# A GRU of two layers followed by a mixture of experts on one core: two parts of the shared expert's inner layer are made at the end of the recurrence, the routing is written out in one fixed order, and small edits are made around both

## The chip, the cores and the metric

The kernel runs on one core of one Trainium2 chip. The metric is the device time of one execution, in microseconds. Each core has five engines: PE (TensorE, matmul, with its weight loads shown apart as PEld), DVE (VectorE), ACT (ScalarE), POOL (GpSimd) and SP (SyncE, which here only starts transfers). Each engine works off its own list of instructions in order.

## The reference, cut to what matters

The input x has 2 sequences of 1024 tokens of 256 numbers. Two layers are added to it, one after the other:

```python
ctx   = cond[:, None, :]
mixed = tanh(x @ W_in.T + b_in + ctx)
h2    = gru(gru(mixed, Wih0, Whh0, ...), Wih1, Whh1, ...)
gate  = sigmoid(cond @ W_gate.T + b_gate)
x     = x + (gate[:, None, :] * h2 + h2) @ W_out.T + b_out

xf     = x.reshape(2048, 256)
shared = silu(xf @ w1) * (xf @ w3) @ w2                 # inner width 512
s      = sigmoid(concat([xf, cond of the row]) @ router_W)       # 8 experts
best   = top_k(s + router_bias, 2)
gates  = s[best] / (sum(s[best]) + 1e-9)   (1/2 each where the sum is <= 1e-9)
routed = sum over the two experts e of gates * gelu(xf @ W1e[e]) @ W2e[e]
out    = x + (shared + routed) / 3
```

## The kernel before, in words

**The recurrence.** Each sequence is cut into chunks that are stepped side by side. The program is a row of *ticks*; in each tick both GRU layers make one step (`step`, inside the class that also has `finish_scanned`, L325-371): matmuls with the recurrent weights (L296), a sigmoid on ACT (L341), a scan on DVE (L344), an elementwise operation (L357), a tanh on ACT (L355), a second scan (L360) and a transpose (L369). Each waits for the one before, so other work is placed by hand into the gaps: `place(tick, where, what)` records a piece of work for a tick and a spot in it ("product" and "behind" on PE, "n0", "scan0", "scan1", "end" for the others), and the main loop (L684-747) takes it out there. When the chunk's state from the warm-up steps is to be dropped, a mask `kept` (L337) is made on DVE inside the step; when the real chunk begins, `start_row` (L484) is transposed for both layers. `front.prepare` (L840-900) makes the gate of the reference, and its sums `ps_gate` (L848) stand in one tick. After the last step `fit` (L495-509) checks for each layer that the chunks fit together; the two results are summed and turned into an integer `count` (L761-764) on which a branch for another, sequential computation hangs; that branch is not taken here.

**Between the two parts.** `front.all_of` (L992-1005) makes the output of the GRU for the last group of tokens: `products` (L914) on PE, `add_x` (L925) on DVE, `route` (L941, the router's sums) on PE, then `turn` (L930, transposes) and `keep` (L952, a copy on ACT).

**The mixture of experts** is `moe` (L1008-1376). Its pieces:

- *Ramps and constants* on POOL (L1037-1072).
- *The routing chain* on DVE (L1081-1218): `raw`, `s` (a sigmoid on ACT), `sel`, then twice `top`, `at`, `place`, `first`, `one`; `both`; two matmuls that count (L1112); `upto` and the `slot` of every token; `low` and `high`; `in_block` and `at_lane`, large one-hot tables of float16; 32 matmuls into `few` (L1171); and `pick` (L1179), the list of token numbers for each block of 128 slots. Beside it stand `mine` to `share` (L1202-1218), the weights of the two experts, and `past` to `words` (L1182-1196), the owner of each block.
- *The shared expert's inner layer* in 16 parts (4 blocks of 512 tokens x 4 slices of 128 inner numbers). A part is `hidden_sums` (L961-970) for w1 and for w3, on PE, two matmuls each of 128x512, and `hidden` (L977-983): `sig` on ACT (L981), `silu` on DVE (L982), and `silu` times the w3 sums on DVE (L983). One part is made ahead of the routing: its w1 sums and half of its w3 sums in the last ticks, the other half as `behind` in `all_of`, its last multiplication after that. EARLY = 8 parts stand beside the routing (a scheduler puts their instructions between those of the routing), one part is filled in at the experts' end (FILL), and the last 6 come in the tail.
- *The experts*: 35 blocks (SURE) of 128 slots. For each, POOL starts an indirect DMA that fetches the block's tokens by `pick` (L1274); PE transposes them (L1237), DVE copies the transpose (L1239), PE multiplies by W1e (L1245), ACT applies gelu (L1285), PE transposes and multiplies by W2e, and the result is stored to `back`. The fetch of block i+3 stands three blocks ahead.
- *The tail*, in an order written by hand (L1353-1376): 8 gathers back (L1335) are started at once, each 128 rows of `back`. Then the 6 parts follow, with two more gathers for each; then 16 output tiles `ps_s` (L1367, four matmuls of 128x256 each), with the last gathers. `add_gone` (L1349) adds the gathered rows with their shares, L1375 adds `ps_s`, L1376 stores the tile. Each gather with an even number is held back by a copy of one element on POOL (L1334), which reads something that is made a little earlier.

Of the kernel before, what the change touches and what calls it, by code (L numbers as in the profile page):

```python
# [18 lines left out]
B = 2  # L19
# [51 lines left out]
EARLY = 8  # L71
# [14 lines left out]
def gru_moe(ctx, tc, xT, vec, bias, w_in, wih0, whh0, wih1, whh1, w_out, w_gate, router, w1, w3, w2, w1e, w2e, out):  # L86
# [62 lines left out]
    class Steps:  # L149
# [177 lines left out]
        def finish_scanned(self, layer, to, tick, before_n, after_n, between, keep=None):  # L327
# [7 lines left out]
            if keep is not None:  # L335
                kept = self.edge.tile([P, U], FP, name=f"kept{layer}")
                nc.vector.tensor_scalar(kept, h, keep, -1.0, ALU.mult, ALU.mult)  # L337
                h = kept
# [14 lines left out]
            n = self.step_pool.tile([P, U, 2], FP, name=f"n{layer}")  # L353
            before_n()
# [46 lines left out]
    with ExitStack() as stack:  # L401
        g = Steps(stack, "", on_pe=False, rest_of_x=rest_of_x)
        g.gates = [
# [138 lines left out]

        def let_wait(ins, copied):


            if ins is not None and copied is not None:
                sync = mybir.DependencyInfo(mybir.DependencyClass.Sync, mybir.DependencyReason.DATA)
                tc.add_manual_dep(ins.ins, copied.ins.name, sync, reason="the next product adds to it")
# [48 lines left out]
        places = {}  # L597

        def place(tick, where, what):
            places.setdefault((tick, where), []).append(what)  # L600

# [42 lines left out]
        place(last_tick - 1, "end", silu)  # L644
        for block in range(1, N // MB):
            place(block, "end", lambda block=block: spread(block))
# [4 lines left out]
        for i, todo in enumerate(front.prepare(g.bank)):  # L651
            for where, what in todo.items():
                place(AHEAD[0] - 8 + i, where, what)
# [32 lines left out]
        with tc.manual_schedule():  # L686
            for tick in range(AHEAD[0] + S + LAG):
                now = [layer for layer in range(2) if runs(layer, tick)]
                for layer in now:
                    if layer not in g.states:  # L690
                        g.states[layer], g.rows[layer] = zero_state, zero_row
                    elif position(layer, tick) == 0:
                        g.starts[layer] = g.states[layer] = begin[layer]
                        g.start_rows[layer] = g.rows[layer] = turned(g.starts[layer], f"start_row{layer}")
# [49 lines left out]
                for layer in now:  # L744
                    if position(layer, tick) == S - 1:
                        fits.append(fit(layer))

            for where in ("n0", "scan0", "end"):
                placed(AHEAD[0] + S + LAG, where)
            front.all_of(  # L750
                g.bank,
                GROUPS // GS - 1,
                lambda: begin_hidden("w3", [1]),
                lambda: nc.vector.tensor_tensor(
                    front.hid(0, slice(0, TB)), begun["silu"], begun["w3"], ALU.mult
                ),
# [13 lines left out]
    with tc.If(n_fit < P):  # L770
        with ExitStack() as stack:
# [46 lines left out]
            front.hidden(0, 0, *(front.hidden_sums(g.bank, 0, 0, name)[0] for name in ("w1", "w3")), *temp)  # L818
# [3 lines left out]
class Front:  # L822
# [17 lines left out]
    def prepare(self, bank):  # L840
# [3 lines left out]
        def gate_sums():  # L844
            ps["gate"] = bank("ps_gate")[:, 0 : KD * B].rearrange("p (k b) -> p k b", b=B)
            for m in range(KD):
                for k in range(KD):
                    last = nc.tensor.matmul(  # L848
                        out=ps["gate"][:, m, :],
                        lhsT=later["w_gate"][:, k, m * P : (m + 1) * P],  # L850
                        rhs=vec_sb[:, COND + k * B : COND + (k + 1) * B],
                        start=(k == 0),
                        stop=(k == KD - 1),
                    )
# [36 lines left out]
        def keep_context():  # L891
# [3 lines left out]
            {"product": gate_sums, "scan1": lambda: spread(0)},  # L895
            {"n0": gates, "scan1": lambda: spread(1)},
# [95 lines left out]
    def all_of(self, bank, group, between=lambda: None, behind=lambda: None):  # L992
# [7 lines left out]
        behind()  # L1000
# [9 lines left out]
def moe(ctx, tc, tag, front, out):  # L1010
# [70 lines left out]
    iota = expert.unsqueeze(1).to_broadcast([P, NT, E])  # L1081
    raw = rt("raw")
    nc.vector.tensor_tensor(raw, logits[:, :, 0:E], context.unsqueeze(1).to_broadcast([P, NT, E]), ALU.add)
    s = rt("s")
    nc.scalar.activation(s, raw, AF.Sigmoid)
    sel = rt("sel")
    nc.vector.tensor_tensor(sel, s, vec_sb[:, RBIAS : RBIAS + E].unsqueeze(1).to_broadcast([P, NT, E]), ALU.add)
    chosen = []
    for i in range(2):
        top = rt(f"top{i}", NT, 1)  # L1090
        nc.vector.tensor_reduce(top, sel, AX.X, ALU.max)
        at = rt(f"at{i}")
        nc.vector.tensor_tensor(at, sel, wide(top), ALU.is_equal)

        place = rt(f"place{i}")
        nc.vector.scalar_tensor_tensor(place, iota, float(E), at, ALU.subtract, ALU.mult)
        first = rt(f"first{i}", NT, 1)
        nc.vector.tensor_reduce(first, place, AX.X, ALU.min)
        nc.vector.tensor_scalar(first, first, float(E), None, ALU.add)
        one = rt(f"one{i}")  # L1100
        nc.vector.tensor_tensor(one, iota, wide(first), ALU.is_equal)
        chosen.append(one)
        if i == 0:
            rest = rt("rest")
            nc.vector.scalar_tensor_tensor(rest, one, -BIG, sel, ALU.mult, ALU.add)
            sel = rest
    both = rt("both", dtype=BF)
    nc.vector.tensor_tensor(both, chosen[0], chosen[1], ALU.add)


    for to, which in ((ps_all.rearrange("p (e t) -> p e t", e=E), every), (ps_before, before)):
        nc.tensor.matmul(out=to, lhsT=which, rhs=both.rearrange("p t e -> p e t"), start=True, stop=True)  # L1112
    upto = rt("upto", E, NT)
    nc.vector.tensor_tensor_scan(
        upto.rearrange("p e t -> p (e t)"), running.rearrange("p e t -> p (e t)"), ps_all, 0.0, ALU.mult, ALU.add
    )

    whole = rt("whole", E, dtype=I32)
    nc.vector.tensor_scalar(whole, upto[:, :, NT - 1], float(P - 1), None, ALU.add)
    nc.vector.tensor_scalar(whole, whole, -P, None, ALU.bitwise_and)  # L1120
    size = rt("size", E)
    nc.vector.tensor_copy(size, whole)
    end = rt("end", E)
    nc.vector.tensor_tensor_scan(end, adding, size, 0.0, ALU.mult, ALU.add)
    slots_taken = rt("slots_taken", 1, dtype=I32)
    nc.vector.tensor_copy(slots_taken, end[:, E - 1 : E])
    start = rt("start", E)
    nc.vector.tensor_tensor(start, end, size, ALU.subtract)

    slot = rt("slot", E, NT)  # L1130
    nc.vector.tensor_tensor(slot, upto, ps_all.rearrange("p (e t) -> p e t", e=E), ALU.subtract)
    nc.vector.tensor_tensor(slot, slot, ps_before, ALU.add)
    nc.vector.tensor_tensor(slot, slot, start.unsqueeze(2).to_broadcast([P, E, NT]), ALU.add)
    slot_of = rt("slot_of", 2, NT)
    for c in range(2):
        own = rt(f"own{c}")
        nc.vector.tensor_tensor(own, chosen[c], slot.rearrange("p e t -> p t e"), ALU.mult)
        nc.vector.tensor_reduce(slot_of[:, c, :].unsqueeze(2), own, AX.X, ALU.add)
    slots = rt("slots", 2, NT, dtype=I32)
    nc.vector.tensor_copy(slots, slot_of)  # L1140
    block = rt("block", 2, NT, dtype=I32)
    nc.vector.tensor_scalar(block, slots, -P, None, ALU.bitwise_and)
    high = rt("high", 2, NT)
    nc.vector.tensor_copy(high, block)
    low = rt("low", 2, NT)
    nc.vector.tensor_tensor(low, slot_of, high, ALU.subtract)

    in_block = rt("in_block", 2, NT, NB, dtype=F16)
    at_lane = rt("at_lane", 2, NT, P, dtype=F16)
    for c in range(2):  # L1150
        nc.vector.tensor_tensor(
            in_block[:, c, :, :],
            block_start.unsqueeze(1).to_broadcast([P, NT, NB]),
            high[:, c, :].unsqueeze(2).to_broadcast([P, NT, NB]),
            ALU.is_equal,
        )
        nc.vector.tensor_tensor(
            in_block[:, c, :, :],
            in_block[:, c, :, :],
            token.unsqueeze(2).to_broadcast([P, NT, NB]),  # L1160
            ALU.mult,
        )
        nc.vector.tensor_tensor(
            at_lane[:, c, :, :],
            lane.unsqueeze(1).to_broadcast([P, NT, P]),
            low[:, c, :].unsqueeze(2).to_broadcast([P, NT, P]),
            ALU.is_equal,
        )
    for c in range(2):
        for t in range(NT):  # L1170
            nc.tensor.matmul(  # L1171
                out=ps_pick,
                lhsT=at_lane[:, c, t, :],
                rhs=in_block[:, c, t, :],
                start=(c == 0 and t == 0),
                stop=(c == 1 and t == NT - 1),
            )
    pick = rt("pick", NB, dtype=I32)
# [272 lines left out]
```

## Time and profile before

| what | value |
|---|---|
| median of the runs | 537.25 us (535.58, 538.12 and 537.25) |
| the profiled execution's own time | 538.56 us |
| its span in the trace | 536.8 us |
| PE busy | 512.1 us, 95% of the span |
| DVE, ACT, POOL busy | 385.1, 243.6, 76.9 us |
| last transpose of the recurrence (L369) | 361.00 to 361.24 us |
| `raw`, the first operation of the routing (L1083) | 365.56 us |
| `both` (L1108), `upto` (L1114), `pick` (L1179) | 372.68, 373.82, 388.06 us |
| first fetch of the experts (L1274) | 388.55 us |
| first product of the experts (L1245) | 396.70 us |
| first gather back (L1335) | 477.65 us |
| last `ps_s` (L1367) ends | 531.13 us |

All times in the lower rows are counted from the start of the span. PE is busy nearly all the time, which says how long PE worked and not whether it had to: a matmul's record begins when PE takes it, and the granted clock of PE is shown apart, in tenths of the full rate. In a row of the timeline, the first number is the start, the second the length, then come the engine, the line, the operation and its tile; what stands in brackets is the idle time before it and what ended that. A view of windows gives for each stretch the busy microseconds of PE, PEld, DVE, ACT and POOL with their numbers of records, then the mean granted clock, the share of the DMA engines and the rate of transfer.

### The profile page before, as it was taken

How to read it: one execution, taken by the hardware profiler on the slowest of the kernel's cores; microseconds unless marked ns; L12 is line 12 of the kernel's file. 1: busy time of each engine (PE TensorE's matmuls, PEld its weight loads, DVE VectorE, ACT ScalarE, POOL GpSimd, SP SyncE). 2: the span in 40 equal slices, each digit the busy share in tenths (PEclk: the TensorE clock that was granted, in tenths of full speed). 3: DMA queues.
4: the chain of work that ended last, by engine and by line, in shares of the span. 5: the costliest groups of instructions: out<-in, count | busy, mean ns of one | idle time of the engine just before them, and what ended most of it. 6: DMA issues, size and time to landing. Idle time of an engine off the chain costs nothing. (4 is left out here: it accounts for less than half of the span.)

```text
span 536.8 us, 18511 instructions
## 1 busy us (share of the span) xinstructions
PE 512.1 (95%) x7492; PEld 341.2 (64%) x7492; DVE 385.1 (72%) x1296; ACT 243.6 (45%) x833; POOL 76.9 (14%) x124
## 2 busy tenths in 40 slices
PE   7999999999999999999999999989999999999795
PEld 4556766666665545665665666654458888854584
DVE  3665789999888888888888888888953333336372
ACT  3444355655665656656666565641133333341000
POOL 1200000000000000000000000002064444037570
PEclk9999999999999999999999999999999999999888
DMA  8980000000000000000000000001024443223252
GB/s 283 373 259 2 2 3 4 3 4 2 4 32 3 12 1 4 2 23 22 3 23 2 23 22 4 22 21 61 1 88 128 120 125 123 70 72 104 81 177 85
DMA packets 23103, 32.13 MB, mean 60 GB/s; under 512 B 3056, under 2 KB 18544, under 8 KB 22992
## 3 DMA queue, kind: packets, MB, share of 16 engines
q1 hardware_dynamic: 17344, 19.94, 11.0%
q0 software_dynamic: 3216, 8.79, 5.8%
q10 hardware_dynamic: 2448, 2.11, 1.2%
q8 instruction: 63, 1.03, 0.8%
q14 instruction: 32, 0.26, 0.2%
HBM read 21.26 MB, written 9.57 MB: 57 GB/s over the span
## 5 line engine op out<-in xcount | busy, mean ns | idle before, releaser
L296 PE MATMUL ps_step<-whh_sb,h 128*32 128x192 f32 x3616 | 193.3, 331 | 5.4 <-DVE h L369 4.2
L296 PEld LDWEIGHTS ps_step<-whh_sb,h 128*32 128x32 f32 x3616 | 94.6, 109 | 71.4 <-DVE h L369 51.9
L360 DVE TENSOR_TENSOR_SCAN row<-gates,n 128x128 f32<-128x128 f32 x230 | 98.0, 426 | 29.6 <-ACT n L355 28.3
L344 DVE TENSOR_TENSOR_SCAN ps_step<-gates,ps_step 128x128 f32<-128x128 f32 x230 | 97.3, 423 | 15.0 <-ACT gates L341 15.0
L268 PE MATMUL ps_step<-wih_sb,h 128*32 128x192 f32 x1696 | 99.7, 328 | 4.1 <-ACT ps_step L526 2.4
L355 ACT ACTIVATE n<-ps_step 128x64 f32<-128x64 f32 x228 | 53.0, 232 | 111.0 <-DVE ps_step L344 110.9
L341 ACT ACTIVATE gates<-ps_step 128x128 f32<-128x128 f32 x230 | 66.5, 289 | 35.5 <-PE ps_step L296 26.0
L268 PEld LDWEIGHTS ps_step<-wih_sb,h 128*32 128x32 f32 x1696 | 57.4, 110 | 26.8 <-ACT ps_step L526 14.5
L369 DVE STREAM_TRANSPOSE h<-row 128x64 f32<-128x64 f32 x230 | 56.5, 246 | 8.0
L969 PE MATMUL ps_w<-x_sb,w_sb 128*128 128x512 f32 x128 | 57.3, 597 | 0.2 <-PEq L1320 0.2
L268 PE MATMUL ps_in<-wih_sb,h 128*32 128x192 f32 x1024 | 54.4, 328 | 1.8 <-ACT h L257 1.4
L1239 DVE COPY hT<-ps_hT 128x256 f32<-128x256 f32 x35 | 14.9, 425 | 49.0 <-PE ps_hT L1237 47.1
L526 ACT COPY ps_step<-inputs 128x256 f32<-128x256 f32 x123 | 47.8, 389 | 0.0
L357 DVE SCALAR_TENSOR_TENSOR n<-gates,row 128x64 f32<-128x64 f32 x224 | 47.0, 210 | 0.0
L268 PEld LDWEIGHTS ps_in<-wih_sb,h 128*32 128x32 f32 x1024 | 34.0, 110 | 14.6 <-issue 4.6
L526 ACT COPY ps_step<-bt 128x256 f32<-128x256 f32 x106 | 39.9, 376 | 3.3
L1274 POOL DMA_INDIRECT inputs<-given,pick x35 | 33.3, 951 | 55.2 <-PE ps_xT L1237 31.9
L969 PEld LDWEIGHTS ps_w<-x_sb,w_sb 128*128 128x128 f32 x128 | 23.6, 190 | 27.1 <-issue 24.7
L1245 PE MATMUL ps_h<-w1e_sb,xT 128*128 x140 | 36.1, 380 | 0.7 <-DVE xT L1239 0.7
L1245 PE MATMUL ps_y<-w2e_sb,hT 128*128 x140 | 36.0, 380 | 0.0
L1335 POOL DMA_INDIRECT inputs<-back,slots x32 | 30.9, 964 | 30.0 <-issue 28.3
L1245 PEld LDWEIGHTS ps_y<-w2e_sb,hT 128*128 128x128 f32 x140 | 26.4, 190 | 4.8 <-DVE hT L1239 1.3
(179 smaller groups left out, 430.9 us busy)
## 6 DMA issues: line engine op xcount, KB each, us to landing
back<-y SPq DMA_DIRECT2D x35, 128.0 KB
w1e_sb<-in_w1e SPq DMA_DIRECT2D x1, 2048.0 KB
w2e_sb<-in_w2e SPq DMA_DIRECT2D x1, 2048.0 KB
given<-inputs SPq DMA_DIRECT2D x8, 256.0 KB
out_dram<-inputs ACTq DMA_DIRECT2D x16, 128.0 KB
whh_sb<-in_whh SPq DMA_DIRECT2D x2, 768.0 KB
x_sb<-in_xT SPq DMA_DIRECT2D x3, 512.0 KB
w_sb<-in_w SPq DMA_DIRECT2D x3, 512.0 KB
```

The source lines that it names most:

```text
L268: last = nc.tensor.matmul(out=out[cols(q), :, :], lhsT=given(k), rhs=self.wih[layer][:, k, q * 3 * U : (q + 1) * 3 * U].rearrange("p (g u) ...
L296: nc.tensor.matmul(out=by_sum(self.sums[layer])[cols(q), 0:3, :], lhsT=self.states[layer][:, k, :], rhs=self.whh[layer][:, k, q * 3 * U : ...
L341: nc.scalar.activation(gates[:, :, :, 1], sums[:, 1:3, :], AF.Sigmoid)
L344: nc.vector.tensor_tensor_scan(s, gates[:, 0, :, :].rearrange("p u i -> p (u i)"), ps[:, 0 : 6 * U : 3], 0.0, ALU.mult, ALU.add,)
L355: nc.scalar.activation(n[:, :, 0], s[:, 1 : 2 * U : 2], AF.Tanh, scale=-1.0 if keep is None else keep)
L357: nc.vector.scalar_tensor_tensor(n[:, :, 1], gates[:, 1, :, 1], 1.0, h, ALU.subtract, ALU.mult)
L360: nc.vector.tensor_tensor_scan(row.rearrange("p u i -> p (u i)"), gates[:, 1, :, :].rearrange("p u i -> p (u i)"), n.rearrange("p u i -> p ...
L369: nc.vector.transpose(to, row)
L526: return nc.scalar.copy(by_sum(banks[layer][tick % 2])[:, 0:4, :], g.sum_bias[1] if layer else inputs[:, group_of(0, tick), :, :],)
L969: last = self.tc.nc.tensor.matmul(out=ps, lhsT=self.later[name][:, k, m * P : (m + 1) * P], rhs=self.x1[:, k, blk * TB : (blk + 1) * TB], ...
L1245: nc.tensor.matmul(out=ps, lhsT=of[:, k, :], rhs=weights_sb[:, bass.ds(e * KD + k, 1), :], start=(k == 0), stop=(k == KD - 1),)
L1274: nc.gpsimd.indirect_dma_start(out=xg, out_offset=None, in_=given[:, :], in_offset=bass.IndirectOffsetOnAxis(ap=pick[:, i : i + 1], axis=0),)
```

## The change

1. **Two parts of the inner layer are made ahead of the routing.** EARLY is 6 and the list of parts begins with the third. Of the first part, the second half of the w3 sums goes into the last tick, and its last multiplication right behind the loop. Of the second part, the first half of the w1 sums stands `between` the output's products and `route`; the rest follows `all_of`, behind the check `fit(1)`, which moves from right behind the last step to behind `all_of`. Six parts stand beside the routing, one at the experts' end and seven in the tail.
2. **The routing and the six parts stand in one hand-written order.** In it ACT makes `sig` and a copy `other` of the w3 sums, DVE makes `silu`, and POOL multiplies `silu` by `other` (on DVE before). `past` to `words` stand behind `pick`. In the source `mine` to `share` stand behind the experts.
3. **Every gather back** from the ninth on is held back by the copy of one element, not only each second one.
4. **In the recurrence**, `kept` is made in a scan slot of the tick before, the transpose `start_row` between two operations of the step, and the sums `ps_gate` are split over two ticks, with `prepare` one tick earlier.

```diff
-EARLY = 8
+EARLY = 6
...
-            if keep is not None:
-                kept = self.edge.tile([P, U], FP, name=f"kept{layer}")
-                nc.vector.tensor_scalar(kept, h, keep, -1.0, ALU.mult, ALU.mult)
-                h = kept
...
+            if h is self.turned_row.get(layer):
+                nc.vector.transpose(h, self.states[layer])
             before_n()
...
+        place(AHEAD[0] - FIRST - 2, "scan1", lambda: mask(0))
+        place(AHEAD[0] + LAG - FIRST - 1, "scan0", lambda: mask(1))
...
+        place(last_tick, "behind", lambda: begin_hidden("w3", [1]))
...
-                place(AHEAD[0] - 8 + i, where, what)
+                place(AHEAD[0] - 9 + i, where, what)
...
-                    if position(layer, tick) == S - 1:
-                        fits.append(fit(layer))
+                    if layer == 0 and position(0, tick) == S - 1:
+                        fits.append(fit(0))
...
-            front.all_of(
-                g.bank,
-                GROUPS // GS - 1,
-                lambda: begin_hidden("w3", [1]),
-                lambda: nc.vector.tensor_tensor(
-                    front.hid(0, slice(0, TB)), begun["silu"], begun["w3"], ALU.mult
-                ),
+            nc.vector.tensor_tensor(front.hid(0, slice(0, TB)), begun["silu"], begun["w3"], ALU.mult)
+
+            def begin_next():
+                begun["next"], _ = front.hidden_sums(g.bank, 0, 1, "w1", None, [0])
+
+            front.all_of(g.bank, GROUPS // GS - 1, begin_next)
+            fits.append(fit(1))
+            front.hidden_sums(g.bank, 0, 1, "w1", begun["next"], [1])
+            pb, _ = front.hidden_sums(g.bank, 0, 1, "w3")
+            front.hidden(
+                0,
+                1,
+                begun["next"],
+                pb,
...
-        def gate_sums():
+        def gate_sums(m):
...
-            {"product": gate_sums, "scan1": lambda: spread(0)},
-            {"n0": gates, "scan1": lambda: spread(1)},
+            {"product": lambda: gate_sums(0), "scan1": lambda: spread(0)},
+            {"product": lambda: gate_sums(1), "scan1": lambda: spread(1)},
+            {"n0": gates},
...
+    def look(i):
+        factors[i] = [wk.tile([P, TB], FP, name=name) for name in ("sig", "silu", "other")]
+        nc.scalar.activation(factors[i][0], begun[i, "w1"], AF.Sigmoid)
+        nc.scalar.copy(factors[i][2], begun[i, "w3"])
+
+    def silu_of(i):
+        (blk, m), (sig, silu, other) = parts[i], factors[i]
+        nc.vector.tensor_tensor(silu, begun[i, "w1"], sig, ALU.mult)
+        nc.gpsimd.tensor_tensor(front.hid(m, slice(blk * TB, (blk + 1) * TB)), silu, other, ALU.mult)
+
+    with tc.manual_schedule():
+        sums_of(0)
...
+            if i == 0:
...
+                look(0)
+                sums_of(1)
+                silu_of(0)
...
+        look(1)
+        sums_of(2)
...
+        silu_of(1)
...
+        look(2)
+        sums_of(3)
...
+            silu_of(2 + c)
+            if c == 0:
+                look(3)
+                sums_of(4)
+        sums_of(5, ("w1",), [0])
...
+        nc.vector.tensor_scalar(pick, ps_pick, float(N - 1), None, ALU.min)
+        look(4)
+        silu_of(4)
+        sums_of(5, ("w1",), [1])
+        sums_of(5, ("w3",))
...
+        look(5)
+        silu_of(5)
+
+    shared_hidden(parts[6:EARLY])
...
-        if behind is not None and i % 2 == 0:
+        if behind is not None:
             nc.gpsimd.tensor_copy(yb[0:1, 0:1], behind[0:1, 0:1])
```

## The prediction

> **What bounds the kernel now.** I read the page's head and its slices first.
>
> ```profile
> PE 512.1 (95%) x7492; PEld 341.2 (64%) x7492; DVE 385.1 (72%) x1296; ACT 243.6 (45%) x833; POOL 76.9 (14%) x124
> PE   7999999999999999999999999989999999999795
> PEclk9999999999999999999999999999999999999888
> ```
>
> PE is busy everywhere, but for two thirds of the span it works inside the recurrence, where DVE's chain sets the pace. The slices show two weak places: the one near slice 28 (about 380 us) and the last three, where the clock is lower too. The chain of waits comes next, here without its first and last pieces:
>
> ```profile
> 476.11 20.84 PE ps_w L969 x48
> 496.95 6.26 PE ps_s L1367 x29
> 503.21 0.46 issue
> ...
> 506.26 1.65 issue
> 507.90 23.23 PE ps_s L1367 x94
> 531.13 0.02 issue
> ```
>
> So the tail ends on PE: 48 records of the inner layer (6 parts), then the output tiles. Between 503 and 508 us PE does little though nothing that it needs is named. The windows of the tail show what follows:
>
> ```profile
> 496.00:504.00 8.00, 7.54 (x34) 6.11 (x33) 0.99 (x2) 0.60 (x1) 5.96 (x8) 1.00 0.35 98
> 504.00:508.00 4.00, 1.30 (x6) 0.82 (x5) 2.15 (x5) 0.00 (x0) 2.09 (x2) 0.83 0.34 100
> 508.00:512.00 4.00, 4.00 (x10) 2.98 (x10) 3.25 (x9) 0.00 (x0) 1.29 (x2) 0.50 0.19 66
> 512.00:516.00 4.00, 4.00 (x16) 3.36 (x16) 3.89 (x10) 0.00 (x0) 3.12 (x5) 0.81 0.60 181
> ```
>
> After the gap the granted clock is 0.50. Sixteen tiles of 1.73 us (8 records at 0.216) would be done at 496.95 + 27.7 = 524.6; they are done at 531.13. This **stall** costs 6.5 us. I do not know its cause: ACT's last `sig` waits 6.7 us for sums that PE took up five microseconds earlier. POOL starts gathers without a pause through that time (5.96 of 8 us busy), but it did so before 494 us without harm.
>
> Last, the timeline of the join of the two layers:
>
> ```profile
> 361.39 2.02 PE L914 MATMUL ps_x<-h,gated_out 128*128 128x128 f32 x16 [1.29 <-DVE h L369]
> 365.56 0.29 DVE L1083 TENSOR_TENSOR raw<-logits,context 128x128 f32<-128x128 f32 x1
> 388.06 0.19 DVE L1179 TENSOR_SCALAR pick<-few 128x39 int32<-128x39 f32 x1
> 388.55 1.18 POOL L1274 DMA_INDIRECT inputs<-given,pick  x1 [19.99 <-DVE pick L1179]
> 396.70 1.13 PE L1245 MATMUL ps_h<-w1e_sb,xT 128*128 x4 [0.68 <-DVE xT L1239]
> ```
>
> The routing takes 22.5 us on DVE, and PE has 8 parts (8 x 3.43 = 27.4 us) to do beside it. PE is done with them at 394.99, when the first fetch has long landed (fetches land 2.3 to 2.7 us after their issue). So **PE's work**, not the routing, starts the experts at 396.70. From there to 476 PE is full (75.96 of 76 us), 2.17 us a block.
>
> **The change part by part.** PE's work stays the same to the matmul; it is moved. So I count idle time of PE.
>
> *Recurrence.* `ps_gate` takes PE 1.05 us at 160.83, and the next step's matmuls begin at 161.81 instead of about 161.43: split in two it fits, 0.4 saved. `kept` (0.21 on DVE, twice, between the transpose and the scan) holds the scan by some 0.13, the two `start_row` transposes (0.20 and 0.24) by about 0.1 each, and they move into gaps. Together -0.8, bounds 0 (other work is displaced) and -1.2 (all of their lengths).
>
> *Last tick.* PE idles 1.29 us before `ps_x`. The second half of the w3 sums (1.02) fits in there and not, as before, between products and `route`; the first half of the second part's w1 sums takes its old place. Products and `route` (364.20) stay; 0.9 us of PE's work is gained.
>
> *Ahead of the routing.* DVE gets `fit(1)` (361.28 to 362.48 before, 1.2 us) between the router's sums and the rest, and behind it `silu` and the product of the second part. PE ends the second part's w1 sums at about 366.1 and its w3 sums at 367.8; `sig` 0.60 and `silu` 0.68 are done by 367.4, the product (0.68) by 368.5. `raw` stands behind it on DVE, and so do the ramps on POOL: **368.55 instead of 365.56, 3.0 later**. Who waits: the whole routing.
>
> *The routing.* From `raw` to `both` it took 7.12 us. Two operations of 128x512 leave that stretch (0.6 each by the steps between starts): 5.9, so `both` at 374.5. In the source `mine` to `share` go behind the experts; in the built program's order they still stand on DVE, nine of them between `both` and `upto`. At about 0.2 each they are past the two counting matmuls (0.7) by 0.8, and `upto` starts near 376.4. From there to `low` the operations hang on each other, 0.28 to 0.33 apart, with one `silu` among them: 4.85, so 381.25. Two pairs of `in_block` (0.72 and 0.72) and `at_lane` (2.2) with a `silu` between give 7.9, the last pick matmuls 0.56: **`pick` at 390.4 instead of 388.06, 2.3 later**. The `past` operations (about 1.1) leave the stretch; that is counted.
>
> *PE beside it.* It has 6 parts. It is through with what stands before the last pick matmuls at 387.1, waits 2.6 us for `at_lane`, and ends the sixth part at 392.8.
>
> *POOL.* This is the part that the profile shows least. POOL takes over the last multiplication of six parts, and four of them stand ahead of the first fetch, the fifth between the first and the second. No row shows this multiplication; nearest is POOL's scaling of a tile of the same 128x512 numbers, with one tile read instead of two:
>
> ```profile
> L204 POOL TENSOR_SCALAR wih_sb<-wih_sb 128x512 f32<-128x512 f32 x1 | 1.5, 1502 | 3.7 <-DMA wih_sb<-in_wih 3.7
> ```
>
> Bounds: 0.68 (what DVE takes) and 3.0 (each tile read at that price). I take 1.5, the nearest row. The fourth starts when its `silu` is done at 390.2, so the first fetch is issued near 392.1 (388.55 before), lands at 394.6; the fifth multiplication puts the second fetch at 395.2, landed at 397.5, and PE needs both blocks transposed before its first product: **398.5 instead of 396.70, +1.8**. With 0.68 and a chain 2 us quicker than I count it is 394.0 (-2.7); with 3.0 each, 402.7 (+6.0). What a DVE operation loses beside POOL is 0.1 to 0.2 in the rows around 367 us (`at` 0.37, elsewhere 0.28) and is inside these bounds.
>
> The Trainium skill's page "SBUF — State Buffer", section "Who interferes with whom", says that a DVE operation with two SBUF inputs and a POOL operation that reads SBUF lock each other out for whole instructions. By that rule each of the three multiplications that stand beside `at_lane` and `in_block` would push the chain by up to its own length, and the sum would be some 4 us higher.
>
> *The clock.* PE now idles 2.6 us before 389.7 and about 5.5 us between 392.8 and 398.5, apart from a few transposes. The row of 504 to 508 us is the only one like it: 1.30 of 4 us busy, and half the clock for the next 6.8 us (506.66 to 513.48), which costs 3.4 us where PE is the bound. Bounds 0 and 3.4. Whether the idle time is long and pure enough is open; I take 1.0.
>
> *Tail.* One part more, PE bound: 8 records at 0.43, **+3.4**. The copy for each gather: gathers then stand 1.43 apart instead of 1.35 in the mean. POOL's row of 32 gathers would end 1.5 + 10 + 24 x 1.43 + about 5 = 50.6 us after its first, PE (7 parts and 16 tiles) after 24.0 + 27.7 = 51.7. So PE's work covers it with 1 us to spare: nothing. Without that cover each 0.08 more per gather costs 2 us. The stall I leave as it is; bounds -6.5 (gone) and +3 (half as much again).
>
> *Sum*, against the profiled execution (span 536.8, own time 538.56): -0.8 + 1.8 + 1.0 + 3.4 = +5.4, a span of 542.2 and a time of 544.0. The profiled execution lies 1.3 above the median of the runs; on the median, 537.25 + 5.4 = **542.7 us**. In a sentence: the tail gets a part back, and the time won for it before the experts is lost in PE's waiting for fetches.
>
> **The rivals.**
>
> *The stall goes* (ends on the other side). Place: 494 to 514 us. For it: POOL's gathers came in bare pairs, and every one now waits for work that is done; the parts there are shifted by 3 us too. Against it: the spacing in the mean hardly changes. Price -6.5: 536.2, or 535.2 if the clock holds. From 5.4 us of relief on, the change is no slower.
>
> *The routing ends earlier than counted*: POOL's multiplication is near 0.68 and the hand order saves more. For it: before, 21 of 23 us of DVE are busy between 364 and 387, and six products leave it. Against it: `raw` is 3 us later, and the long one-hot tables (7.3 us) stay. Then the experts start at 394.0: 542.7 - 4.5 - 1.0 = 537.2. Together with the stall's end: 530.7.
>
> *POOL and DVE hinder each other*, or POOL's product takes 3.0: the first product at 402.7, and the clock falls: 542.7 + 4.2 + 2.4 = 549.3.
>
> **How the numbers follow.** About 0.5%, 2.7 us, is what a measurement can tell from no change: faster is below 534.6, slower above 539.9. My forecast 0.39 (its own range 540 to 545.5); the stall goes alone 0.18 (0.10 faster, 0.08 same); the routing quicker alone 0.10 (0.02 faster, 0.05 same, 0.03 slower); both 0.13 (faster); POOL hinders 0.20 (slower). So faster 0.25, same 0.13, slower 0.62. The range 531 to 549 takes in nearly all of the forecast and of the rivals that stand alone.
>
> **What would show it.** In the changed kernel: `raw` near 368.5, `pick` near 390.4, POOL's multiplications at 1.5 us, the first fetch near 392, the first product near 398.5, all less 0.8; the granted clock below 1.00 just behind 398; 56 records of the inner layer in the tail; and a gap of PE with ACT's `sig` waiting some 5 to 7 us in the last 40 us. I am wrong if the experts start before 396, if the tail has no such gap, or if a multiplication on POOL takes over 2 us.

## The result, and the profile after

The changed kernel takes 543.87 us in the median of five runs (543.68 to 544.51), the one before 537.25 in five runs beside them (535.58 to 538.83): ratio 1.0118, 95% interval 1.0098 to 1.0139: slower by 1.2%. The profiled execution has a span of 542.1 us; 542.7 was forecast for the median and 542.2 for the span. One thing has to be known for what follows: the runs were made in groups, and the kernel before itself took 536 to 538 us in three of them and 531.7 to 531.9 in two others. So each ratio below holds for its group (the changed kernel itself ran in the first alone), and absolute times are compared only where that is said.

The page's slices after the change, against those shown for before:

```profile
PE   7999999999999999999999999999689999989995
PEclk9999999999999999999999999999979999999999
```

The weak place near slice 28 is now deeper (6 and 8, where it was 9 and 8), the clock drops there, and the tail's three digits went from 795 to 995: the end has lost its gap, the middle has gained one. The chain of waits (start, length, what) says the same of the end:

```profile
483.51 24.27 PE ps_w L992 x56
507.79 7.55 PE ps_s L1430 x35
...
515.35 1.10 PE ps_s L1430 x4
516.46 0.32 issue
516.78 19.46 PE ps_s L1430 x89
```

Seven parts (56 records) take 24.27 us, and sixteen tiles end at 536.24, which is 0.75 us later than without any gap. Before, the same sixteen tiles lost 6.5. The timeline of the join shows where the middle gets late:

```profile
360.51 2.02 PE L937 MATMUL ps_x<-h,gated_out 128*128 128x128 f32 x16 [0.39 <-DVE logits L979]
367.68 0.29 DVE L1137 TENSOR_TENSOR raw<-logits,context 128x128 f32<-128x128 f32 x1
372.11 1.38 POOL L1131 TENSOR_TENSOR inputs<-silu,other 128x512 f32<-128x512 f32 x1 [1.43 <-ACT other L1126]
372.27 1.36 DVE L1147 TENSOR_TENSOR at<-rest,top 128x128 f32<-128x128 f32 x1
...
379.97 1.28 POOL L1131 TENSOR_TENSOR inputs<-silu,other 128x512 f32<-128x512 f32 x1 [6.48 <-DVE silu L1130]
380.14 0.29 DVE L1198 TENSOR_REDUCE slot_of<-own 128x16 f32<-128x128 f32 x1
380.35 1.13 DVE L1197 TENSOR_TENSOR own<-one,slot 128x128 f32<-128x128 f32 x1
...
387.55 1.33 POOL L1131 TENSOR_TENSOR h<-silu,other 128x512 f32<-128x512 f32 x1 [6.30 <-DVE silu L1130]
387.79 1.75 DVE L1219 TENSOR_TENSOR in_block<-in_block,token 128x624 f16<-128x624 f16 x1
...
392.49 1.27 POOL L1131 TENSOR_TENSOR h<-silu,other 128x512 f32<-128x512 f32 x1 [3.61 <-DVE silu L1130]
392.55 0.20 DVE L1246 TENSOR_SCALAR pick<-few 128x39 int32<-128x39 f32 x1 [0.21 <-PE few L1238]
...
393.93 1.22 POOL L1315 DMA_INDIRECT inputs<-given,pick  x1 [0.17 <-issue]
...
400.76 1.62 PE L1286 MATMUL ps_h<-w1e_sb,xT 128*128 x3 [0.94 <-DVE xT L1280]
```

`ps_x` and `raw` come where they were forecast (367.68 for 368.55 less 0.8). From there the first three of POOL's multiplications each have a DVE row beside them that is 0.8 to 1.1 us too long (`at`, `own`, `in_block`), while `slot_of`, which reads one tile and not two, keeps its 0.29 us beside the second. `pick` is 3 us later than forecast, and the first product comes at 400.76, 4.1 us later than before. What PE waited for between 386 and 486 us (total, times, longest):

```profile
PE few L1238 <- DVE at_lane L1225: 4.4, 1, 4.4
PE ps_w L992 <- DVEq L1383: 1.4, 1, 1.4
PE ps_xT L1278 <- DMA inputs<-given,pick: 1.4, 2, 1.0
PE ps_h L1286 <- DVE xT L1280: 0.9, 1, 0.9
PE ps_y L1286 <- DVE hT L1280: 0.4, 1, 0.4
```

First the tables of the routing, then the fetches. The windows (busy PE, PEld, DVE, ACT, POOL, then the granted clock) show what the waiting does to the clock:

```profile
386.00:392.00 6.00, 1.64 (x25) 0.94 (x24) 5.96 (x6) 1.18 (x2) 1.33 (x1) 0.87 0.01 4
392.00:398.00 6.00, 5.64 (x23) 2.25 (x20) 5.22 (x9) 0.90 (x2) 4.84 (x5) 0.56 0.10 22
398.00:404.00 6.00, 4.05 (x13) 2.96 (x14) 1.27 (x3) 1.95 (x3) 5.02 (x5) 0.72 0.29 87
```

PE is busy 1.64 of 6 us, and the clock halves twice: for most of 392 to 398, and again at the start of the experts.

### The profile page after: what moved, and what is told of

It reads as the page before. It is cut to its first block, busy times and chain, and to the rows that moved or that the text cites. A ratio compares the mean times of both kernels' runs of the same rounds, so it can differ in the third digit from the quotient of the medians.

```text
span 542.1 us, 18554 instructions
## 1 busy us (share of the span) xinstructions
PE 513.3 (95%) x7492; PEld 341.3 (63%) x7492; DVE 389.2 (72%) x1290; ACT 247.4 (46%) x839; POOL 88.7 (16%) x142
## 3 DMA queue, kind: packets, MB, share of 16 engines
q8 instruction: 63, 1.03, 0.8%
## 5 line engine op out<-in xcount | busy, mean ns | idle before, releaser
L992 PE MATMUL ps_w<-x_sb,w_sb 128*128 128x512 f32 x128 | 59.9, 618 | 1.4 <-DVEq L1383 1.4
L1286 PE MATMUL ps_h<-w1e_sb,xT 128*128 x140 | 37.6, 392 | 0.9 <-DVE xT L1280 0.9
L1398 POOL DMA_INDIRECT inputs<-back,slots x32 | 32.2, 1006 | 29.3 <-issue 26.6
L1326 ACT ACTIVATE he<-ps_h 128x256 f32<-128x256 f32 x35 | 13.5, 385 | 36.4 <-PE ps_h L1286 33.5
```

The lines of the kernel that those rows point to most:

```text
L992: last = self.tc.nc.tensor.matmul(out=ps, lhsT=self.later[name][:, k, m * P : (m + 1) * P], rhs=self.x1[:, k, blk * TB : (blk + 1) * TB], ...
L1286: nc.tensor.matmul(out=ps, lhsT=of[:, k, :], rhs=weights_sb[:, bass.ds(e * KD + k, 1), :], start=(k == 0), stop=(k == KD - 1),)
```

## The experiments

Each is told with its edit and with what was put down before it ran. Ratios are those against the kernel before in the same group of runs.

**POOL's multiplication put back on DVE** (a_dve):

```diff
-        nc.gpsimd.tensor_tensor(front.hid(m, slice(blk * TB, (blk + 1) * TB)), silu, other, ALU.mult)
+        nc.vector.tensor_tensor(front.hid(m, slice(blk * TB, (blk + 1) * TB)), silu, other, ALU.mult)
```

> The changed kernel, with the last multiplication of the six parts beside the routing on DVE again (still from the copy that ACT makes). Theory C (beside POOL's multiplication a DVE operation with two inputs stands still: at, own and the multiplication of in_block took 1.36, 1.13 and 1.75 us instead of 0.28, 0.37 and 0.80; and POOL's list holds the first two fetches): at, own and in_block go back to their short times, pick comes at 391.5 to 392 (three multiplications of 0.6 take the place of 2.8 lost), the first fetch at once behind it near 392.2 instead of 393.9, the first product near 397.2 instead of 400.8, the time 539 to 540.5 us. Theory D (the long rows have another cause, and the start of the experts hangs on the chain of DVE alone): pick 1.8 later near 394.4, first product near 400, time 543 to 544 us.

Measured: 540.80 us, ratio 1.0052 (1.0035 to 1.0069) against 1.0118. The timeline, with POOL empty:

```profile
373.30 0.29 DVE L1147 TENSOR_TENSOR at<-rest,top 128x128 f32<-128x128 f32 x1
...
387.77 0.81 DVE L1219 TENSOR_TENSOR in_block<-in_block,token 128x624 f16<-128x624 f16 x1
...
392.09 0.19 DVE L1246 TENSOR_SCALAR pick<-few 128x39 int32<-128x39 f32 x1
...
392.57 1.18 POOL L1315 DMA_INDIRECT inputs<-given,pick  x1 [21.92 <-DVE pick L1246]
```

`at` is back from 1.36 to 0.29 us and the multiplication of `in_block` from 1.75 to 0.81. Theory C holds: three multiplications on DVE cost the chain less than what it lost beside POOL. `pick` is just 0.5 us earlier, but the first fetch follows at once and the second is at 394.06 and not at 396.62; the first product is at 398.19, 2.6 us earlier, where 3.6 was expected. The time lies just above the 539 to 540.5 us of theory C: behind nine fetches in a row (392.57 to 402.82) PE then waits 1.81 us at 404 for its own results, which the experiments on late sums below come back to.

**The shares moved for real** (a_share). In the changed kernel the lines from `mine` to `share` stand behind the experts in the source, and their instructions between `both` and `upto`. Here the block stands inside the hand-written order:

```diff
         nc.vector.tensor_copy(words, word.rearrange("p w i -> p (w i)"))
+        mine = rt("mine", 2, NT)
...
+        nc.vector.tensor_scalar(share, share, 1.0 / 3.0, None, ALU.mult)
```

> The changed kernel, with the operations mine to share moved in the source to right behind words, so that they really stand behind pick on DVE. Theory E (nine to eleven of them hold upto by 0.8 to 1.2 us): upto near 375.8 instead of 376.9, pick and the first product 0.8 to 1.2 earlier, 542.8 us. Theory F (the chain has slack there, POOL's multiplications decide): the first product within 0.3 of 400.8, 543.9 us.

Measured: 542.19 us, ratio 1.0072 (1.0055 to 1.0089). `upto` at 375.42, `pick` at 390.96, the first product at 399.31: 1.45 us earlier than in the changed kernel, of which 0.4 lies ahead of the routing. Theory E holds, at the upper end of its size.

**The copies ahead of the gathers**, taken out of the changed kernel (a_unpaced) and put into the kernel before (b_paced), by the same line:

```diff
-        if behind is not None and i % 2 == 0:
+        if behind is not None:
```

> The changed kernel, with only each second gather held back, as before. Theory A: the stall comes back, PE idles some 4 us in the tail and its clock halves after it, 543.9 + 5.5 = 549.4 us. Theory B: the tail stays as it is, from PE's first matmul in it (483.5) to the last output tile some 52.7 us, 543.9 us within 1.

> The kernel before, with one edit of the change: every gather back from the ninth on is held back by the copy of one element, not each second one. Theory A (the 6.5 us stall of the tail comes from gathers that POOL starts in bare pairs): the stall shrinks to about 1 us, so 537.2 - 5.5 = 531.7 us, last output tile near 525.5. Theory B (the stall went in the changed kernel because its tail has one part more and starts 7 us later; the copy has nothing to do with it): PE still idles near 503 to 508 us and the time stays at 537 us, within 1.

Measured: a_unpaced 543.13 us, ratio 1.0090 (1.0073 to 1.0107); b_paced 536.16 us, ratio 0.9971 (0.9952 to 0.9991). The chain of a_unpaced:

```profile
483.07 24.27 PE ps_w L992 x56
507.34 27.64 PE ps_s L1430 x128
```

All 128 records of the output stand in one piece: without the copies the changed kernel has no gap at all. So theory A fails for the changed kernel, which does not need the copies. In b_paced, PE's tail is 4.6 us shorter than before (475.48 to 525.88, against 476.11 to 531.13), so there they do help; but the last gather is now issued at 522.79, the last addition follows it, and only 1.6 of the 5.5 us that were expected reach the time (by the ratio).

**Where the late sums come from.** In the tail of the kernel before, results of PE are taken up long after they were made:

```profile
490.04 0.18 POOL L1334 COPY inputs<-sig 1x1 f32<-1x1 f32 x1
490.25 0.60 ACT L981 ACTIVATE sig<-ps_w 128x512 f32<-128x512 f32 x1 [2.08 <-DVE h L983]
...
500.23 0.60 ACT L981 ACTIVATE sig<-ps_w 128x512 f32<-128x512 f32 x1 [6.71 <-PE ps_s L1367]
...
508.65 0.42 DVE L1375 SCALAR_TENSOR_TENSOR inputs<-ps_s,inputs 128x256 f32<-128x256 f32 x1 [2.43 <-remote]
```

Part of this is a wait that the program makes. `sig` has two buffers, and POOL's copies (L1334) read it, so ACT's third to fifth `sig` of the tail start within 0.03 us of the end of the copy of two parts earlier (the fourth: 490.04 + 0.18, then 490.25). The last `sig` is another case: its copy ended at 495.57, and it came at 500.23. The first output tile was done at about 498.7 and was added at 508.65, after DVE had stood idle for 2.43 us. PE's own stops lie inside the fourth and fifth output tiles (from 503.21 to 507.90), where the profile names nothing that it waits for.

In the kernel before, the gathers from the ninth on are left out (b_nogather), or all 32 are replaced by plain transfers of as many bytes, started by SP (b_direct). In both, the sums of the routed part take other rows than the reference's.

```diff
-        nc.gpsimd.indirect_dma_start(
-            out=yb,
...
+        nc.sync.dma_start(out=yb, in_=back[i * P : (i + 1) * P, :])
```

> The kernel before without the gathers back from the ninth on and without the copies that hold them back: 24 of 32 are left out, and the sums take what stands in their buffers. Theory G (PE's sums are seen late because POOL starts gathers without a pause): ACT's sigmoids in the tail follow their sums by at most 1.5 us, PE has no gap, the last output tile is done at 476.1 + 20.8 + 27.7 = 524.6, the time is 532 us or a little less. Theory K (the late sums have nothing to do with the gathers): the gap at 503 to 508 us stays, 537 us.

> The kernel before with each of the 32 gathers back replaced by a plain transfer of 128 rows in order, started by SP, without the copies on POOL: as many bytes, other rows. Theory G1 (it is POOL's starting of gathers): no late sums and no gap, 531 to 532.5 us. Theory G2 (it is the traffic into the buffers or the additions that wait for it): late sums and the gap stay, 536 to 538 us.

Measured: b_nogather 531.91 us, ratio 0.9915 (0.9883 to 0.9948); b_direct 531.87 us, ratio 0.9903 (0.9870 to 0.9935). In b_direct ACT's sigmoids of the last parts follow their sums like a clock, 3.43 us apart, and the output has no gap:

```profile
490.87 0.60 ACT L981 ACTIVATE sig<-ps_w 128x512 f32<-128x512 f32 x1 [2.84 <-PE ps_w L969]
494.30 0.60 ACT L981 ACTIVATE sig<-ps_w 128x512 f32<-128x512 f32 x1 [2.84 <-PE ps_w L969]
```

```profile
475.15 20.84 PE ps_w L969 x48
495.98 27.64 PE ps_s L1360 x128
```

The last part's sigmoid comes at 494.30; in the kernel before, whose tail starts 0.96 us later, it came at 500.23, so 5.0 us late. Theory K falls: without POOL's gathers the late sums are gone, in all nine runs of the two kernels (533.14 us at most, the kernel before 534.82 at least). G1 and G2 are not told apart as cleanly as was planned, because SP starts most of the transfers long before the tail. Between 396 and 476 us:

```profile
inputs<-back SPq DMA_DIRECT2D x27, 128.0 KB
```

So b_direct takes out of the tail not only POOL's starting but also most of the traffic, and the copies too. What speaks against the traffic by its amount is the stretch in which those 27 transfers run: 174 GB/s, beside POOL's fetches, and PE is busy all the time, where the tail of the kernel before moved 98 GB/s ahead of its gap.

```profile
400.00:440.00 40.00, 40.00 (x224) 35.01 (x222) 14.06 (x38) 13.96 (x37) 16.93 (x18) 1.00 0.60 174
```

Against the copies speak b_paced, with twice as many of them and a shorter gap, and the next experiment. POOL's starting of gathers is thus the likelier cause, but it was not tried with the same traffic at the same time.

**One part fewer beside the routing** (b_seven), and with the change's recurrence and last tick (b_best):

```diff
-EARLY = 8
+EARLY = 7
```

> The kernel before with EARLY = 7: one part fewer beside the routing and seven in the tail; nothing else. Theory B (the stall of the tail costs nothing once seven parts stand in it, since PE then has work behind the late sums for longer; the copies have nothing to do with it): the first product 3.0 to 3.4 us earlier than 396.7, the tail 24.3 + 27.7 = 52 us from its first matmul, in all 537.2 - 5.7 = 531.5 us. Theory H (what took the stall away in the changed kernel lies elsewhere: its later start of the tail, or POOL's multiplications): a gap of PE and half a clock in the last 40 us as before, 537 us, within 1.

> The kernel before with EARLY = 7, the change's edits of the recurrence (kept, start_row, ps_gate, prepare one tick earlier), and the second half of the first part's w3 sums in the last tick; the routing, POOL's work and the gathers as before. Under theory B: 0.9 us less than with EARLY = 7 alone for the recurrence and the last tick each at most, so 530 to 531 us. Under theory H: 535.5 to 536.5 us.

Measured: b_seven 537.42 us, ratio 1.0015 (0.9999 to 1.0030); b_best 535.29 us, ratio 0.9966 (0.9947 to 0.9985). The times are those of theory H (535.29 is 0.2 us below its range), the tail is nearer to theory B: in b_seven it lost 2.0 us and not 6.5 (476.81 to 530.76, of which 51.9 are work), so the seventh part does help, as far as one trace of each says. But a like lateness turned up at the start of the experts, where no copy stands and where POOL could now start nine fetches in a row (387.89 to 398.13):

```profile
398.43 1.08 PE L1245 MATMUL ps_h<-w1e_sb,xT 128*128 x4
400.73 0.38 ACT L1285 ACTIVATE he<-ps_h 128x256 f32<-128x256 f32 x1 [4.32 <-PE ps_h L1245]
400.85 0.42 DVE L1239 COPY hT<-ps_hT 128x256 f32<-128x256 f32 x1 [2.52 <-PE ps_h L1245]
...
401.32 1.95 PE L1245 MATMUL ps_y<-w2e_sb,hT 128*128 x4 [1.82 <-DVE hT L1239]
```

The first product was 2.9 us earlier (393.80), and PE then waited 1.8 us for its own results and ran at half clock behind that (1.95 us for four records, usually 1.03). The wait goes with the length of the row of fetches: 1.82 us behind nine (here) and 1.81 behind nine (a_dve), 1.15 behind eight (b_best), none in the kernel before, where the fetches stood in rows of five and four with 1.35 us between them.

**Fewer buffers for the fetches, and gathers spread out** (c_away3, c_best, c_best8):

```diff
-AWAY = 5
+AWAY = 3
...
-BACK = 8
+BACK = 4
...
-            fetch_back(base[:, j - 1, :] if j else None)
+            fetch_back(base[:, j - 2, :] if j > 1 else None)
```

> The kernel of b_best (before, with EARLY = 7, the change's recurrence and last tick) with AWAY = 3: three buffers instead of five for the fetched blocks, so that POOL can start at most three fetches in a row before it has to wait for a transpose. Theory G1 at the experts' start (b_best has PE waiting 1.2 us for a copy that waits for PE near 400 us, behind eight fetches without a pause): no wait of PE for hT there, experts 2 us shorter, 533.3 us. If three buffers are too few: PE waits for fetches, 536 us or more.

> As with AWAY = 3, and the gathers back spread out: 4 at once instead of 8, every later one held back by the copy, those of the output loop by the tile two before, the additions one tile later. Theory G1: POOL rests now and then, PE's sums are seen in time, no gap in the tail: 1 us less than with AWAY = 3 alone, 532.3 us. Other way: the last gathers come late and the end waits for them, 535 us.

> The kernel before (EARLY = 8, AWAY = 5) with the change's recurrence and last tick and the gathers spread out: 6 at once, every later one held back, those of the output loop by the tile two before, the additions one tile later. Theory G1: 0.35 + 0.9 for recurrence and last tick, 5 to 6 for the stall: 530.5 to 531.5 us. If the tail's gathers are still too dense: 534 to 535 us.

Measured: 532.69, 532.68 and 533.63 us. The first two times are near those expected, the third is over 2 us above its range, and none says much of its edit: the kernel before took 531.92 in the same group (20 runs, 531.28 to 532.48), so the ratios are 1.0014 (1.0003 to 1.0025), 1.0016 (1.0006 to 1.0025) and 1.0037 (1.0023 to 1.0051). In this group there was no lateness to take away. In c_away3, POOL starts gathers through 497 to 514 us with hardly a pause, and the output tiles are added in time from the first on. None of the three beats the kernel before there. In c_best8 the last addition waits 1.6 us for its gather, so with nothing late, gathers that are spread out only delay the end.

**The changed kernel with plain transfers** (a_direct), the counterpart of b_direct; the same edit, and here too the sums take other rows.

> The changed kernel with each of the 32 gathers back replaced by a plain transfer of 128 rows in order, started by SP, without the copies on POOL: the counterpart of b_direct (531.87 us), so that neither has POOL's gathers in the tail. If the change's later start of the experts, its wait ahead of the tail and its one part more are a price that the end of the stall only hid: 4.1 + 2.1 + 1.3 + 3.4 = 10.9 us more than b_direct, 542.7 us, tail of 24.3 + 27.7 = 52 us without a gap. If these times shrink when POOL is free in the tail, so that the change is near neutral without the stall: 533 to 537 us.

Measured: 542.36 us, ratio 1.0201 (1.0184 to 1.0218) against a kernel before at 531.65. The chain:

```profile
483.45 24.27 PE ps_w L992 x56
507.72 27.64 PE ps_s L1423 x128
```

10.5 us more than b_direct (which ran in another group), where the sum of the terms gave 10.9. So the price of the change does not shrink when POOL is free in the tail: without the late sums it is 2%. The changed kernel with its gathers was not run in a group without late sums.

## Why the forecast held, point by point

The number was right by luck. The stall, which the forecast left as it was, went (5.7 us less), and three terms were larger than forecast (3.1, 1.1 and 1.3 us, together 5.5 more). By the forecast's own sign ("I am wrong ... if the tail has no such gap") its account of the tail was wrong. In the profiled pair (forecast, then measured, in us):

| term | forecast | measured | from |
|---|---|---|---|
| up to the end of the recurrence | -0.8 | -0.9 | last transpose 361.00 to 360.12 |
| from there to the first product | +1.8 | +4.9 | 35.70 to 40.64 |
| first product to the end of the experts | +1.0 | +2.1 | 77.38 to 79.45 |
| ahead of the tail | 0 | +1.3 | 2.03 to 3.30, from the start of PE's last sums of the filled-in part |
| one part more | +3.4 | +3.4 | 24.27 for 20.84 |
| the stall of the tail | 0 | -5.7 | 6.47 to 0.75 lost |
| behind the last tile | 0 | +0.2 | 5.7 to 5.9 |
| sum | +5.4 | +5.3 | 536.8 to 542.1 |

- *Recurrence.* 0.9 in this pair, but 0.37 of it is that the first scan started earlier (10.51 for 10.88). From first to last scan the five traces with the old recurrence took 349.24 to 349.66, mean 349.42, the nine with the new one 348.89 to 349.42, mean 349.05. So its edits are worth 0.4 and not 0.8: the term was mis-sized.
- *Last tick and `raw`.* Right: the gap ahead of `ps_x` went from 1.29 to 0.39, and `raw` came at 367.68 (forecast 367.75).
- *The routing.* The step "a DVE operation loses 0.1 to 0.2 beside POOL" failed. `at` lost 1.08 us, the second `own` 0.76 and the multiplication of `in_block` 0.95, together 2.8 of the 3.0 by which `pick` missed its forecast (392.55 for 389.6). The row that I read for that price, `at` at 367.08, stood beside an operation of POOL of 0.21 us (a cast at 367.09), too short to cost more. a_dve shows the cause: with POOL empty all three rows are back at their short times. (The forecast's time for `pick` was not the sum of the terms shown either: 381.25 + 7.9 + 0.56 is 389.7 and not 390.4, so by the terms the miss is 3.6.) The page "SBUF — State Buffer" of the Trainium skill, section "Who interferes with whom", has the rule that the forecast set aside: a DVE operation with two SBUF inputs and a POOL operation that reads SBUF exclude each other for the whole instruction. The rows agree: `at` began 0.16 us behind POOL's multiplication and ended 0.14 behind it.
- *POOL.* The price of its multiplication was near (1.27 to 1.38 us for 1.5), and so was the order: the first two fetches stood behind it. The first fetch was in use 4.0 us after its issue (393.93 to 397.96) where 2.5 was taken, but the first product waited for the second (issued at 396.62, in use at 399.38).
- *Shares between `both` and `upto`.* Right in kind (a_share): 0.8 forecast, 1.1 measured (1.45 less the 0.4 ahead of the routing).
- *The clock.* Half the clock did come, and cost more than the 1.0 taken: 3.4 us at half rate at the start of the experts (below) lost 1.7, and 0.4 of a wait for `hT` makes up the 2.1 of the table. The earlier half-rate stretch, between 392 and 398, cost little, since PE was through with the sixth part at 397.61 and waited another 0.35 for the fetch.
- *Ahead of the tail.* Not forecast. In the changed kernel PE waits 1.43 us and starts the tail at 483.51, 0.32 behind the end of a table load on ACT (483.19); in the kernel before it waits 0.15 and starts at 476.11, while that load still runs (475.48 to 476.76). The wait of 1.43 stands in all traces with the new recurrence but a_dve, whose sums have the same order and which has 0.15. What PE waits for there is open: the profile names only DVE's queue.
- *The tail's part and the copies.* Right: 3.4 us, and the copies gain nothing in the changed kernel (a_unpaced, which is no slower without them). The forecast's sum for POOL's row of gathers gives 50.8 and not 50.6, which changes nothing.
- *The stall.* The step "the stall I leave as it is" failed; it was the first rival, at a chance of 0.18, that came true together with a piece of the third. The reason I gave for that rival (gathers in bare pairs) is not what made the difference: without the copies the changed kernel has no gap either, though in the kernel before they cut the loss from 6.5 to 1.9 us (b_paced).

The clock at the start of the experts, in windows of one microsecond (first number after the window: PE busy; behind POOL's: the granted clock):

```profile
400.00:401.00 1.00, 0.24 (x1) 0.28 (x2) 0.28 (x1) 0.00 (x0) 0.70 (x2) 0.84 0.25 57
401.00:402.00 1.00, 1.00 (x3) 0.82 (x4) 0.00 (x0) 0.00 (x0) 0.99 (x2) 0.50 0.21 82
...
404.00:405.00 1.00, 1.00 (x8) 0.90 (x7) 0.17 (x1) 0.38 (x1) 0.90 (x1) 0.95 0.44 131
```

From 0.84 in the first window to 0.95 in the last, the half rate lasts 3.4 us (0.32 + 3 + 0.1). The page "TensorE: Matmul & The Clock Gate" of the Trainium skill, section "Part 1: The HAM clock gate (the "warmup" mystery)", gives a window of about 3.4 us for it, and the rows agree.

What is shown of the stall: it goes when POOL's gathers go (b_direct, b_nogather), and PE's finished sums are taken up late behind long rows of POOL's indirect transfers (b_seven, a_dve). That PE then stops because it is too far ahead of what has been taken up is a reading and was not tried. Six parts lost 6.5 us, with all the copies 1.9; kernels with seven parts lost 0 to 2.0 (a_unpaced 0, a_share 0.5, the changed kernel 0.75, b_best 1.1, a_dve 1.35, b_seven 2.0), so the small loss of the changed kernel goes with its seventh part, as far as one trace of each says. What stays open is why. By their times, two groups of runs had none of it with the same gathers, and in the traces of c_away3, c_best and c_best8 the tail has no gap; one of these groups and one with the stall ran on the same chip, seven minutes apart. So POOL's gathers are needed for it but not enough, and no run here varied what else it takes. This also means that the ratio of 1.0118 is not a property of the two kernels alone: with the late sums gone on both sides it is 1.02 (1.0201 in the group of a_direct; a_direct over b_direct, from two groups, 542.36 / 531.87 = 1.0197).

## What to carry to other kernels

Moving the elementwise work of one engine to another pays only if both can work at the same time: look at which operands they read, and measure one pair side by side before a whole chain is planned on it. When work is taken from beside a dependent chain, the chain becomes the bound, and a wait of PE can cost again through the clock (here 3.4 us at half rate lost 1.7). And a gap in a profile that nothing explains should be tested first, since a forecast that carries it along as a constant has an error of its whole size.

## What the runs showed of the hardware

- Beside POOL's multiplication of two tiles of 128x512 (1.27 to 1.38 us) a DVE operation with two operands in SBUF took 1.13 to 1.75 us where it takes 0.29 to 0.81 with POOL empty (`at`, `own`, `in_block`); one with a single operand (`slot_of`) kept its 0.29.
- With POOL starting eight or nine indirect fetches 1.25 to 1.49 us apart, PE waited 1.15 to 1.82 us for results of its own that ACT and DVE took up late (b_best, b_seven, a_dve). In the tail of the kernel before, behind 22 gathers, the first output tile (taken up at 496.95, 1.73 long) was added at 508.65, with DVE idle for the last 2.43 us before. With 24 of the 32 gathers left out (b_nogather) or all replaced by plain transfers, most of them ahead of the tail (b_direct), the tail had no gap; by their times, two of the five groups of runs had none either.
- The granted clock fell to one half in stretches of 3.4 us or twice that, each behind a stretch in which PE was partly idle (before: 1.30 of 4 us busy; b_seven: a wait of 1.82). A wait of 1.81 us in a_dve was followed by none.
